# Four of sixteen input loads over fifteen DMA engines, issued from GpSimd, in a store-bound bilinear kernel

## Chip, cores, metric

One core of a Trainium2 chip. The metric is the device time of one execution in microseconds.

## The reference

```python
# r_inputs: (4096, 32, 64) f32,  W: (496, 64, 64) f32
idx_i, idx_j = np.triu_indices(32, k=1)
vi = inputs[:, idx_i, :]
vj = inputs[:, idx_j, :]
vidots = jnp.einsum('bpd,pde->bpe', vi, W)
return vidots * vj                     # (4096, 496, 64) f32
```

The output has 520 MB, the inputs 42 MB.

## The kernel before

A block is 256 batch rows, two on each of 128 partitions; there are sixteen. TensorE multiplies, VectorE (or ACT and GpSimd together) multiplies by the field and fills one of three output buffers `ot`, SP stores it. The next block's input goes into one of two buffers `xs`, issued by ACT for all but the first two blocks:

```python
    xpool = ctx.enter_context(tc.tile_pool(name="xpool", bufs=2))
    opool = ctx.enter_context(tc.tile_pool(name="opool", bufs=3))
    ...
    def load_x(blk, eng, k0=0, k1=NB):
        src = rows_of(x, blk).rearrange("(p k) f d -> p (k f) d", k=NB)
        eng.dma_start(out=xs[blk][:, 1 + k0 * F : 1 + k1 * F, :], in_=src[:, k0 * F : k1 * F, :])
    ...
        if s in loads:
            new_x(loads[s])
            load_x(loads[s], nc.scalar)
    ...
            nc.sync.dma_start(out=...[:, kt, n0 : pa + m, :], in_=ot[:, n0 - base : pa + m - base, :])
```

## Time and profile before

| | before |
|---|---|
| time, median of three runs | 1354.09 us (1353.96 to 1354.46) |
| TensorE, VectorE, GpSimd busy | 87%, 71%, 39% |
| mean DMA rate | 416 GB/s |
| period of a block with an x load, by the last landing record | 82.7 us |
| period of a block without one | 77.9 us |
| sixteenth behind fifteenth landing record, median of the stores issued from 430 to 1250 us | 4.8 us |

The last three rows come from the trace's landing records. Each of the 182 transfers of the kernel before leaves sixteen of them (2912 in all), read here as one for each of the core's sixteen DMA engines, made when that engine's share has landed. They carry no engine number, but their spread tells whether one engine is behind: the sixteenth record's distance from the fifteenth is called the lag below. The profile lines themselves are in the prediction.

### The profile page before, as it was taken

To read this page: it belongs to the slowest core of one execution; us is meant where nothing else is said; L and a number is where in the kernel's file an instruction comes from. 1 tells how busy PE (TensorE), PEld (TensorE's weight loads), DVE (VectorE), ACT (ScalarE), POOL (GpSimd) and SP (SyncE) were. 2 spreads that over 40 slices of the span, in tenths; PEclk is the share of its full clock that TensorE was granted. 3 is DMA by queue.
4 is the path that set the end of the run, shared out by engine and by line. 5 is a ranking of instruction groups with operands and counts; after the bars stand their busy time and mean duration, and the time that the engine had idled before them with its cause. 6 is when DMAs were issued, how large, how long until landed. Compare 5 with 4: busy or idle time off the path is not lost.

```text
span 1353.3 us, 17856 instructions
## 1 busy us (share of the span) xinstructions
PE 1180.3 (87%) x7424; PEld 690.9 (51%) x7424; DVE 956.9 (71%) x1262; ACT 374.1 (28%) x367; POOL 530.2 (39%) x246
## 2 busy tenths in 40 slices
PE   6989889889799897988879989888987989988994
PEld 4556545545455454555445545454554545545552
DVE  5778768767677676776757777676775767767774
ACT  3432222222232232222222222222222222223221
POOL 1813424444243443433444334433434434344431
PEclk9989999989999898999989999899998999989997
DMA  9999999999999999999999999999999999999997
GB/s 386 370 426 408 424 427 431 428 432 431 418 414 419 433 412 418 422 413 426 428 407 422 417 425 410 423 421 407 425 410 426 419 422 427 401 432 428 415 417 319
DMA packets 26273, 562.92 MB, mean 416 GB/s; under 512 B 2912, under 2 KB 2912, under 8 KB 3040
## 3 DMA queue, kind: packets, MB, share of 16 engines
q1 hardware_dynamic: 24048, 530.59, 92.4%
q10 hardware_dynamic: 2144, 31.20, 5.5%
q8 instruction: 58, 0.95, 0.3%
q14 instruction: 23, 0.19, 0.0%
HBM read 41.68 MB, written 520.09 MB: 415 GB/s over the span
## 4 chain that ended last, share of the span: by engine, by line
DMA 50%; PE 25%; DVE 17%; POOL 3%; issue 2%; ACT 0%; DVEq 0%; SPq 0%; POOLq 0%; ACTq 0%
DMA out_dram<-ot 50%; PE ps L211 20%; DVE ot L228 17%; PE ptx L114 4%; POOL ot L226 3%; PE ptw L104 1%; DMA raw<-in_L_rec_W_dram 1%; ACT tmp L225 0%; DVE rp L95 0%; POOL rp L95 0%; DVEq L228 0%; ACT wT L107 0%; SPq L76 0%; POOLq L226 0%; SPq L233 0%
## 5 line engine op out<-in xcount | busy, mean ns | idle before, releaser
L228 DVE TENSOR_TENSOR ot<-ps,xs 128x1024 f32<-128x1024 f32 (+15 forms) x1252 | 945.6, 808 | 364.7 <-DMA out_dram<-ot 185.9
L211 PE MATMUL ps<-wT,xT 64*128 64x512 f32 (+13 forms) x6272 | 1034.9, 473 | 132.8 <-DVE ot L228 121.3
L211 PEld LDWEIGHTS ps<-wT,xT 64*128 64x128 f32 x6272 | 563.7, 197 | 569.9 <-DVE ot L228 306.8
L226 POOL TENSOR_TENSOR ot<-tmp,xs 128x1024 f32<-128x1024 f32 x220 | 519.6, 2362 | 647.4 <-ACT tmp L225 457.1
L225 ACT COPY tmp<-ps 128x1024 f32<-128x1024 f32 x220 | 222.7, 1012 | 500.1 <-PE ps L211 459.6
L118 ACT COPY xT<-ptx 128x1024 f32<-128x1024 f32 x128 | 129.6, 1012 | 428.2 <-PE ptx L114 428.2
L114 PE MATMUL ptx<-ident,xs 128*128 128x128 f32 x1024 | 141.2, 281 | 18.5 <-DVE ot L228 9.9
L114 PEld LDWEIGHTS ptx<-ident,xs 128*128 128x128 f32 x1024 | 111.0, 142 | 64.3 <-issue 44.1
L72 POOL MEMSET xs<- 128x64 f32 x16 | 2.4, 152 | 148.6 <-DVE ot L228 148.6
L104 PE MATMUL ptw<-ident,rp 128*128 128x128 f32 (+1 forms) x128 | 19.2, 305 | 3.9 <-DVE rp L95 3.9
L104 PEld LDWEIGHTS ptw<-ident,rp 128*128 128x128 f32 (+1 forms) x128 | 16.2, 160 | 10.3 <-DVE rp L95 5.0
L107 ACT COPY wT<-ptw 128x1024 f32<-128x1024 f32 (+1 forms) x15 | 14.8, 984 | 21.4 <-PE ptw L104 21.4
L95 DVE COPY rp<-raw 128x1024 f32<-128x1024 f32 (+1 forms) x9 | 10.7, 1219 | 11.1 <-DMA raw<-in_L_rec_W_dram 11.1
L95 POOL COPY rp<-raw 128x1024 f32<-128x1024 f32 x4 | 8.0, 1994 | 0.1
L95 ACT COPY rp<-raw 112x1024 f32<-112x1024 f32 (+1 forms) x3 | 5.9, 1959 | 5.1 <-POOL ot L226 3.3
L107 DVE COPY wT<-ptw 128x1024 f32<-128x1024 f32 x1 | 1.2, 1224 | 3.3 <-PE ptw L104 3.3
L118 ACT ACT_TABLE_LOAD x1 | 1.3, 1283 | 0.7 <-PEq L251 0.7
masks.py:197 POOL MEMSET ident<- 128x128 f32 x1 | 0.2, 206 | 0.3 <-POOLq L251 0.3
masks.py:199 POOL TENSOR_SCALAR_AFFINE_SELECT ident<-ident 128x128 f32<-128x128 f32 x1 | 0.3, 295 | 0.0
L251 POOL MEMSET const-float32-0.0<- 128x1 f32 x1 | 0.1, 99 | 0.2 <-issue 0.2
L251 POOL MEMSET const-bfloat16-1.0<- 128x1 bf16 x1 | 0.1, 102 | 0.0
L251 POOL MEMSET const-uint8-127<- 128x1 uint8 x1 | 0.1, 102 | 0.0
(1 smaller groups left out, 0.1 us busy)
## 6 DMA issues: line engine op xcount, KB each, us to landing
out_dram<-ot SPq DMA_DIRECT2D x64, 3360.0 KB, 16.2
out_dram<-ot SPq DMA_DIRECT2D x32, 3168.0 KB, 15.4
out_dram<-ot SPq DMA_DIRECT2D x32, 3104.0 KB, 17.0
out_dram<-ot SPq DMA_DIRECT2D x31, 2880.0 KB, 16.4
xs<-in_r_inputs_dram ACTq DMA_DIRECT2D x14, 2048.0 KB, 16.6
raw<-in_L_rec_W_dram SPq DMA_DIRECT2D x3, 2048.0 KB, 14.3
xs<-in_r_inputs_dram SPq DMA_DIRECT2D x2, 1024.0 KB, 10.9
xs<-in_r_inputs_dram SPq DMA_DIRECT2D x1, 2048.0 KB, 24.6
```

The source lines that it names most:

```text
L72: nc.gpsimd.memset(xs[blk][:, 0, :], 0.0)
L95: copy(rp[:r], src[:, k * EU : (k + 1) * EU])
L104: nc.tensor.transpose(pt[:, n, :r], rp[:r, n].rearrange("p h d -> p (h d)"), ident[:r, :r])
L107: copy(wT[c][:, :, k * EU : (k + 1) * EU], pt[:, :, :r].rearrange("p e r -> p r e"))
L114: nc.tensor.transpose(pt[:, n, :], xs[blk][:, s : s + 2, :].rearrange("p f d -> p (f d)"), ident)
L118: copy(xT, pt)
L211: nc.tensor.matmul(ps[:, h, lo - pa : hi - pa, :], xT[blk, kt, n // RUN][h * D : (h + 1) * D, n % RUN, :], wT[c][h * D : (h + 1) * D, lo - ...
L225: nc.scalar.copy(tmp, src)
L226: nc.gpsimd.tensor_mul(dst, tmp, xj)
L228: nc.vector.tensor_mul(dst, src, xj)
L251: nc = _bacc.Bacc("TRN2", target_bir_lowering=False, num_devices=1)
```

## The change

The intent is to relieve one of the sixteen DMA engines. 120 of a block's 128 rows go through GpSimd's queue, in two halves by field. The small transfers (`turn_engines`) are there so that the same engine is left out each time. The last eight rows go through ACT's queue, five and three.

No record carries an engine's number, so the numbers in the texts are names. Followed from packet to packet, where the next one starts 3 to 4 ns before the end of the last, the three rows lie in all four loads on three of the engines that carry the five. These three are called 0 to 2, the other two 3 and 4. Number 15 is the name for the engine that 120 rows from ACT's queue are taken to leave out (e4); 5 to 14 are the rest.

```diff
+    SWR = 120
 ...
+    def turn_engines(k: int):
+        n = k if k > 1 else 17
+        c = used[0] % 8
+        used[0] += 1
+        src = x[: NB * n].rearrange("(p k) f d -> p k f d", k=NB)
+        tc.keep_in_program_order(
+            nc.gpsimd.dma_start(out=scratch[:n, :, c : c + 1], in_=src[:, :, 0, 0:1])
+        )
+    def load_fifteen(blk: int):
+        rows = rows_of(x, blk).rearrange("(p k) f d -> p k f d", k=NB)
+        dst = xs[blk][:, 1:, :].rearrange("p (k f) d -> p k f d", k=NB)
+        for a, b in ((SWR, SWR + 5), (SWR + 5, P)):
+            nc.scalar.dma_start(out=xs[blk][a:b, 1:, :], in_=rows[a:b].rearrange("p k f d -> p (k f) d"))
+        for h in range(2):
+            cut = slice(h * F // 2, (h + 1) * F // 2)
+            tc.keep_in_program_order(
+                nc.gpsimd.dma_start(out=dst[:SWR, :, cut, :], in_=rows[:SWR, :, cut, :])
+            )
+            turn_engines(1)
 ...
     load_x(1, nc.sync)
+    turn_engines(5)
 ...
-            load_x(loads[s], nc.scalar)
+            if loads[s] % 3 == 1:
+                load_fifteen(loads[s])
+            else:
+                load_x(loads[s], nc.scalar)
 ... (end of the kernel)
+    turn_engines(11)
```

## The prediction

> **What bounds the kernel now.** I read the page first, then the table by stage, the waits of the store queue, GpSimd's timeline at a block's start, and last the landing records in the trace (each transfer leaves sixteen, one for each DMA engine).

> ```profile
> PE 1180.3 (87%) x7424; PEld 690.9 (51%) x7424; DVE 956.9 (71%) x1262; ACT 374.1 (28%) x367; POOL 530.2 (39%) x246
> ...
> DMA  9999999999999999999999999999999999999997
> ...
> q1 hardware_dynamic: 24048, 530.59, 92.4%
> q10 hardware_dynamic: 2144, 31.20, 5.5%
> ...
> DMA 50%; PE 25%; DVE 17%; POOL 3%; issue 2%; ACT 0%; DVEq 0%; SPq 0%; POOLq 0%; ACTq 0%
> ...
> xs<-in_r_inputs_dram ACTq DMA_DIRECT2D x14, 2048.0 KB, 16.6
> ```

> The DMA engines are busy everywhere, the compute engines are not, and half of the chain that ended last is output transfers. The stores (q1) take 92.4% of the DMA time, the fourteen loads of ACT's queue (q10) 5.5%. So the bytes set the time, and the question is how evenly the sixteen engines carry them.

> ```profile
> 265.00:348.00 83.00, 73.37 (x454) 42.71 (x454) 58.74 (x78) 22.27 (x22) 33.19 (x15) 0.94 1.01 430
> 348.00:431.00 83.00, 72.94 (x462) 43.19 (x464) 58.97 (x80) 22.27 (x22) 33.18 (x15) 0.94 0.99 420
> 431.00:514.00 83.00, 74.14 (x458) 42.86 (x458) 58.99 (x78) 22.27 (x22) 33.18 (x15) 0.94 0.99 418
> ```

> The last two columns are the DMA share and GB/s, one row for each of three blocks of 256 batch rows. In the first the engines never run dry and move 430 GB/s; afterwards they move 418 to 420. The landing records say why. In stores issued between 100 and 200 us the sixteenth record comes a median 0.23 us after the fifteenth; between 200 and 300 us it is 2.3 us, from 430 us on it stays near 4.8 us, while the first fifteen lie within 1.8 us. One engine is slower. Its backlog grows until an output buffer (three) waits for it; then the other fifteen run dry for about 1.1 us in each block (area under the packet records). The slow engine never rests: its landings are evenly spaced by bytes. From its last landings a block with an x load takes 82.7 us (nine of the last ten such blocks within 0.1) and the only later block without one takes 77.9. So **on that engine an x load costs 4.8 us**, its eight rows of 16 KB. A block moves 34.6 MB (32.5 out, 2.1 in); at 430 GB/s the other fifteen would need 80.5 us. They have 2.2 us to spare in each block.

> ```profile
> 348.68 0.15 POOL L72 MEMSET xs<- 128x64 f32 x1 [9.98 <-DVE ot L228]
> 352.08 2.36 POOL L226 TENSOR_TENSOR ot<-tmp,xs 128x1024 f32<-128x1024 f32 x1 [3.25 <-ACT tmp L225]
> 358.62 2.35 POOL L226 TENSOR_TENSOR ot<-tmp,xs 128x1024 f32<-128x1024 f32 x1 [4.17 <-DMA out_dram<-ot]
> ```

> The new GpSimd transfers stand between the first two rows (the instruction order of the changed kernel shows it): there GpSimd waits 3.25 us now, and again 4.17 us before the next product.

> [...] Before, every transfer has 128 or 112 rows and sixteen records[...] This trace has one slow engine with no GpSimd transfer at all, and does not name it.[...]

> **The change, part by part.** Blocks 4, 7, 10 and 13 are loaded in the new way.
> - *Removed:* four loads of 128 rows. The slow engine loses 4 x 4.8 = 19.2 us if it is the one left out.
> - *Added, GpSimd:* twice 120 rows of 4 KB by 2. [...]eight rows on each of fifteen engines, none on the sixteenth. The transfer behind has 17 rows[...]
> - *Cost of the small ones:* 34 elements of 4 bytes on the spared engine. The 4-byte packets in the trace take 9 ns, so 0.3 us of engine time[...]
> - *Added, ACT:* five and three rows, on engines 0 to 4 and 0 to 2. Engines 0 to 2 carry two extra rows, 2 x 0.61 = 1.2 us (x packets take 611 ns): 80.5 + 1.2 = 81.7 us in such a block, still under 82.7. Two issues of 0.35 us instead of one; ACT is 28% busy.
> - *GpSimd's time:* four transfers[...]. 4 to 6 us where it waits 3.25 now: the first product is 1 to 3 us late, four times. The slow engine has some 5 us more queued than the others then, and the next product waits for a buffer anyway: nothing on the path.
> - *The slower landing:* 4 KB packets taking turns with 26.9 KB stores. 32 rounds of 0.15 + 1.0 us are 37 us against 16.6; the next use is some 70 us off. Hidden.

> Sum: 19.2 less 4 to 8, less 1 to 2 for block 4, which is loaded when the backlog is only 2.5 us and cannot give all of 4.8: 9 to 14 us, middle 12.5. 1354.1 - 12.5 = 1341.6, rounded to **1341**. The design closes well: a spared block cuts the backlog by about 4 us, two plain blocks restore 2 x 2.2.

> **The rivals.**
> *The wrong engine is spared.* [...] If the slow engine isn't the spared one, it keeps its eight rows and nothing is won: 1353 to 1357. One in four.
> *The small transfers[...] eat the gain.* If 34 elements cost 2.4 us, two of them take the 4.8 saved: about 1354. The 9 ns speak against it.
> *GpSimd becomes the path.* It is 39% busy, but in-order; if a transfer costs it 3 us or more, its first product is 9 us late in four blocks, more than the backlog: up to 4 x 4 us lost, 1345 to 1360. Its waits of 3.25 and 4.17 us speak against it.
> *More is won.* All bytes at 430 GB/s take 562.9 / 0.430 = 1309 us, plus some 25 us of start: 1334 is the floor with even engines.

> **Range and chances.** If the slow engine is spared (three in four), 1335 to 1348; if not, around 1355. That gives 1333 to 1357. Faster by over 2% means under 1327, below the floor: 0.02. Slower by over 2%, above 1381, takes a stall that none of these sizes gives: 0.03.

> **What would show it.** Right: GpSimd's queue as a third row of the DMA queues with about 7.9 MB; ACT's down by that much; the gap between fifteenth and sixteenth record falls by some 4 us after a spared load and recovers over two blocks; those blocks take 78 to 79 us by last landing, the others 82.7. Wrong: the gap stays near 4.8 us everywhere (another engine is spared), or the spared blocks take 82 us with the gap gone (fifteen engines or GpSimd bound), or GpSimd's first product comes over 5 us late and the store behind it with it.

## The result

The changed kernel takes 1345.61 us (four runs, 1345.58 to 1345.65) against 1354.28 us (four runs). The ratio is 0.9936 (95% interval 0.9919 to 0.9953), 8.7 us less. A ratio here is the mean of one kernel's runs over that of the other's in the same rounds, so not quite the ratio of the medians. By the 2% rule the verdict is "same"; the two sets of times do not overlap.

From the page of the changed kernel, the DMA queues and two groups of GpSimd:

```profile
q1 hardware_dynamic: 24048, 530.59, 93.0%
q10 hardware_dynamic: 1632, 23.33, 4.2%
q0 software_dynamic: 2496, 7.88, 1.5%
...
L92 POOL DMA_DIRECT2D scratch<-in_r_inputs_dram x10 | 9.1, 908 | 0.2 <-issue 0.2
...
L103 POOL DMA_DIRECT2D xs<-in_r_inputs_dram x8 | 6.0, 753 | 1.4 <-issue 1.4
```

GpSimd's queue is the new third row, with the 7.88 MB that ACT's has lost, and issuing the 18 transfers occupies GpSimd for 15.1 us in all. Its timeline at the second of the four loads:

```profile
511.03 0.15 POOL L72 MEMSET xs<- 128x64 f32 x1 [10.04 <-DVE ot L261]
511.54 0.76 POOL L103 DMA_DIRECT2D xs<-in_r_inputs_dram  x1 [0.35 <-issue]
512.30 0.99 POOL L92 DMA_DIRECT2D scratch<-in_r_inputs_dram  x1
513.28 0.74 POOL L103 DMA_DIRECT2D xs<-in_r_inputs_dram  x1
514.02 0.96 POOL L92 DMA_DIRECT2D scratch<-in_r_inputs_dram  x1
515.00 2.37 POOL L259 TENSOR_TENSOR ot<-tmp,xs 128x1024 f32<-128x1024 f32 x1
```

The four issues fit into the wait that stood there before: the first product starts 3.97 us after the memset did, where it was 3.40 us. GpSimd is 0.6 us late, once per load.

The landing records show the aim being met. The two columns are medians of the sixteenth record's lag over the stores issued 50 to 12 us ahead of a load and 25 to 60 us behind it:

| load issued at | lag ahead of it | lag behind it |
|---|---|---|
| 265 us | 1.9 us | 0.8 us |
| 512 us | 4.9 us | 1.3 us |
| 757 us | 4.6 us | 1.4 us |
| 1004 us | 3.8 us | 1.6 us |

By last landing, three consecutive blocks (the spared load and two ACT loads) now take 245.9 to 246.6 us (the shortest: 84.7 + 82.6 + 78.6), where they took 3 x 82.7 = 248.1. A single block's period says little: a GpSimd load lands over some 42 us, all of it behind the boundary at which one period ends, so one block looks short and the next long.

But not everything is gained. In the 46 us behind each load, these are the stages of the changed kernel at three of the four loads; ahead of them one of its ordinary ACT loads (last columns: DMA share, GB/s), and last the kernel before at the same three loads:

```profile
428.00:474.00 46.00, 39.55 (x240) 22.83 (x240) 31.00 (x42) 11.14 (x11) 16.66 (x8) 0.93 1.00 426
510.00:556.00 46.00, 39.61 (x258) 22.63 (x258) 33.55 (x47) 12.47 (x13) 20.74 (x13) 1.00 1.00 412
756.00:802.00 46.00, 39.71 (x256) 22.76 (x258) 33.63 (x47) 12.37 (x13) 20.93 (x13) 1.00 1.00 409
1003.00:1049.00 46.00, 39.68 (x254) 22.42 (x252) 33.53 (x44) 12.15 (x12) 21.41 (x13) 1.00 1.01 413
...
514.00:560.00 46.00, 38.97 (x244) 22.57 (x244) 31.07 (x43) 11.14 (x11) 16.69 (x8) 0.93 0.99 418
762.00:808.00 46.00, 38.84 (x242) 21.82 (x240) 30.87 (x41) 11.14 (x11) 16.68 (x8) 0.96 0.99 421
1010.00:1056.00 46.00, 38.62 (x240) 22.62 (x242) 29.91 (x42) 11.13 (x11) 16.67 (x8) 0.93 0.98 411
```

In the changed kernel the engines never run dry in either kind, but while fifteen of them carry a load they move 409 to 413 GB/s instead of 426 at the three later loads. (At the first, issued at 265 us, where the slow engine has little backlog yet, it is 423.) The kernel before moves 411 to 421 there, with engines that run dry (share 0.98 to 0.99).

Over the whole execution this costs little. The durations of all packet records, added up and divided by sixteen, say how long an engine works on average:

| | span, us | mean busy time of an engine, us | mean idle time, us |
|---|---|---|---|
| before | 1353.3 | 1329.7 | 23.6 |
| the change | 1343.8 | 1330.6 | 13.2 |
| e3 (below) | 1341.9 | 1330.2 | 11.7 |

The work has grown by 1 us at most; the whole gain is idle time that is gone. Successive records of one engine overlap by some 3.5 ns; with that taken off, between 265 and 1250 us an engine is idle for 12.6 us before, 4.3 in the changed kernel and 2.6 in e3. That is the limit which the prediction's sum did not have.

### The profile page after: what moved, and what is told of

Same layout as the page of the kernel before. It is cut to its first block, busy times and chain, and to the rows that moved or that the text cites. A ratio compares the mean times of both kernels' runs of the same rounds, so it can differ in the third digit from the quotient of the medians. Undisturbed runs are those within 1.5% of the kernel's fastest.

```text
span 1343.8 us, 17902 instructions
## 1 busy us (share of the span) xinstructions
PE 1163.9 (87%) x7424; PEld 680.1 (51%) x7424; DVE 956.0 (71%) x1262; ACT 374.1 (28%) x367; POOL 544.7 (41%) x264
## 2 busy tenths in 40 slices
DMA  9999999999999999999999999999999999999997
## 3 DMA queue, kind: packets, MB, share of 16 engines
q1 hardware_dynamic: 24048, 530.59, 93.0%
q0 software_dynamic: 2496, 7.88, 1.5%
## 4 chain that ended last, share of the span: by engine, by line
DMA 50%; PE 23%; DVE 16%; POOL 6%; issue 3%; ACT 1%; DVEq 0%; SPq 0%; POOLq 0%; ACTq 0%
DMA out_dram<-ot 50%; PE ps L244 18%; DVE ot L261 16%; POOL ot L259 5%; PE ptx L143 4%; PE ptw L133 1%; DMA raw<-in_L_rec_W_dram 1%; POOL scratch L92 1%; ACT tmp L258 1%; POOL xs L103 0%; DVE rp L124 0%; POOL rp L124 0%; DVEq L261 0%; ACT wT L136 0%; POOL xs L72 0%
## 5 line engine op out<-in xcount | busy, mean ns | idle before, releaser
L244 PE MATMUL ps<-wT,xT 64*128 64x512 f32 (+13 forms) x6272 | 1017.8, 467 | 122.4 <-DVE ot L261 110.7
L244 PEld LDWEIGHTS ps<-wT,xT 64*128 64x128 f32 x6272 | 552.7, 193 | 553.1 <-DVE ot L261 289.0
L72 POOL MEMSET xs<- 128x64 f32 x16 | 2.4, 151 | 148.5 <-DVE ot L261 148.5
L92 POOL DMA_DIRECT2D scratch<-in_r_inputs_dram x10 | 9.1, 908 | 0.2 <-issue 0.2
L103 POOL DMA_DIRECT2D xs<-in_r_inputs_dram x8 | 6.0, 753 | 1.4 <-issue 1.4
## 6 DMA issues: line engine op xcount, KB each, us to landing
xs<-in_r_inputs_dram ACTq DMA_DIRECT2D x10, 2048.0 KB, 17.3
raw<-in_L_rec_W_dram SPq DMA_DIRECT2D x3, 2048.0 KB, 17.1
```

Source lines behind the costliest of these rows:

```text
L72: nc.gpsimd.memset(xs[blk][:, 0, :], 0.0)
L92: nc.gpsimd.dma_start(out=scratch[:n, :, c : c + 1], in_=src[:, :, 0, 0:1])
L103: nc.gpsimd.dma_start(out=dst[:SWR, :, cut, :], in_=rows[:SWR, :, cut, :])
L244: nc.tensor.matmul(ps[:, h, lo - pa : hi - pa, :], xT[blk, kt, n // RUN][h * D : (h + 1) * D, n % RUN, :], wT[c][h * D : (h + 1) * D, lo - ...
```

## Experiments

Theory A: the gain comes from leaving out the one slow engine. Theory B: it comes from GpSimd's path itself, whose 4 KB packets let stores go first. Each diff is against the changed kernel unless it says otherwise. "Before" was run with every batch (1354.3 to 1355.3 us).

| run | edit | time, us | ratio to before |
|---|---|---|---|
| the change | | 1345.61 | 0.9936 |
| e1 | another engine left out | 1358.51 | 1.0027 |
| e2 | GpSimd, all 128 rows | 1354.87 | 0.9997 |
| e3 | ACT's rows four and four | 1342.98 | 0.9912 |
| e4 | the 120 rows from ACT | 1357.87 | 1.0021 |
| e5, e6 | needless loads | 1409.69, 1410.71 | 1.0405, 1.0412 |
| e7 | e3 with whole rows | 1360.43 | 1.0039 |
| e8 | e3 with seven blocks | 1344.82 | 0.9923 |
| e9 | e3 in four parts | 1343.01 | 0.9915 |
| e10 | e3 cut by batch row | 1357.20 | 1.0019 |
| e11 | e3, last eight rows by GpSimd, whole | 1352.94 | 0.9988 |
| e12 | e11, the eight rows cut by field | 1343.70 | 0.9917 |

**e1: leave out another engine.**

```diff
-    turn_engines(5)
+    turn_engines(6)
-    turn_engines(11)
+    turn_engines(10)
```

> Six rows instead of five in the first small transfer (and ten in the last)[...]. Theory A (the gain comes from leaving out the one slow engine): the gain is lost, 1353 to 1357 us, and the gap between fifteenth and sixteenth landing record stays near 4.8 us. Theory B (the gain comes from GpSimd's path itself, 4 KB packets that let the stores go first): 1345 to 1347 us as now.

Measured 1358.51 us, and the lag stays at a median 4.5 us. One row more in the first small transfer turns a gain of 8.7 us into a loss of 3.6. Most of the loss fits too, by an estimate: if the slow engine is number 4, it now gets eight rows from GpSimd and still one from ACT, nine instead of eight, and 4 x 0.6 = 2.4 us (a 16 KB packet takes 0.61 us). Theory B falls.

**e2: GpSimd without sparing.** `SWR = 128`, no small transfers, no ACT transfer.

> The same four blocks loaded by GpSimd with all 128 rows on sixteen engines, no small transfers, nothing by ACT. Theory A: 1353 to 1357 us, like before or a little slower. Theory B: 1344 to 1347 us.

Measured 1354.87 us, ratio 0.9997, lag 4.9 us. Issuing from GpSimd in 4 KB packets neither costs nor gains anything that shows (95% interval 0.9982 to 1.0012). Its stages at the same three loads:

```profile
514.00:560.00 46.00, 39.53 (x244) 22.45 (x242) 31.89 (x42) 12.02 (x12) 17.98 (x9) 0.96 1.00 419
762.00:808.00 46.00, 39.41 (x244) 22.32 (x242) 31.77 (x42) 11.90 (x12) 17.98 (x9) 0.96 1.00 420
1010.00:1056.00 46.00, 39.23 (x244) 22.11 (x244) 31.31 (x43) 11.14 (x12) 18.14 (x10) 0.96 1.01 424
```

419 to 424 GB/s (426 at the first load), so GpSimd's queue alone explains little of the fall.

**e3: take ACT's row off engine 4.**

```diff
-        for a, b in ((SWR, SWR + 5), (SWR + 5, P)):
+        for a, b in ((SWR, SWR + 4), (SWR + 4, P)):
```

> ACT's eight rows as four and four (engines 0 to 3) instead of five and three (0 to 4 and 0 to 2). If the slow and spared engine is number 4[...], it loses its last row: 4 x 0.6 us, 1343.0 to 1343.6 us. If it is another engine, engine 3 gets one row more and nothing changes: 1345.3 to 1346.0 us.

Measured 1342.98 us, 2.6 us less than the change (3.2 by the ratios, each with its own batch of "before"), as expected if the slow engine is number 4. The edit moves one row from ACT's first transfer to its second. So one 16 KB row on engine 4 costs 0.65 to 0.8 us of the whole time in each load, and the engine that GpSimd leaves out is the slow one. No later version is faster. (e1 to e8 ran on chip 0 by their records, e9 to e11 on chip 3 and e12 on chip 2: the same sparing paid on all three.)

**e4: the 120 rows from ACT's queue**: the same two half transfers issued by `nc.scalar`, no small ones. That they lie on fifteen engines, as GpSimd's do, is taken to be so and not shown.

> The 120 rows issued from ACT's queue[...], no GpSimd transfer. If the slow engine is number 15: 1335 to 1344 us, better than with GpSimd. If not: 1353 to 1357 us, no gain, engines 0 to 2 carry two more rows.

Measured 1357.87 us: nothing is won, so if an engine is left out here, it is not the slow one. Engine 4 would then carry nine rows as in e1 (an estimate: eight of the 120 and one of ACT's five), and they lose 3.0 and 3.6 us. The stages:

```profile
514.00:560.00 46.00, 38.92 (x244) 22.17 (x244) 31.20 (x43) 11.14 (x11) 16.65 (x8) 0.96 0.99 407
762.00:808.00 46.00, 40.87 (x242) 23.18 (x244) 30.92 (x44) 11.35 (x12) 16.66 (x8) 0.89 0.99 400
1012.00:1058.00 46.00, 39.83 (x240) 22.28 (x240) 30.48 (x41) 11.13 (x11) 16.66 (x8) 0.93 0.99 405
```

The same fall of the rate, to 400 to 407 GB/s (422 at the first load), without any GpSimd transfer; a small part of it is engines running dry (share 0.99). It goes with the loads of 120 rows, not with who issues. The nine rows on engine 4 would be a second difference from e2, so this is not shown apart from them.

**e5 and e6: needless loads of four or five rows**, added to the kernel before, to name the slow engine in a second way:

```diff
             load_x(loads[s], nc.scalar)
+            nc.scalar.dma_start(
+                out=raw[3][:4, :],            # e6: [:5, :]
+                in_=rows_of(x, loads[s]).rearrange("(p k) f d -> p (k f d)", k=NB)[:4],
+            )
```

> The kernel before with one needless transfer of four rows of 16 KB behind each of ACT's fourteen x loads[...]. If the slow engine is number 4, these four have 2.2 us to spare in each block and 0.6 us more is hidden: 1354 to 1356.5 us. If the slow engine is one of 0 to 3: about 14 x 0.6 = 8.5 us more, 1362 to 1364 us.

> The same with five rows[...]. If the slow engine is number 4: 14 x 0.6 = 8.5 us more than before, 1361 to 1365 us. If it is any of 5 to 15: as with four rows, within 1 us.

Both failed as experiments: 1409.69 and 1410.71 us. Nothing in the program held the copies in their places, so the scheduler put all fourteen at the front of ACT's queue, where thirteen of them take 55.08 us. From ACT's timeline of e5:

```profile
87.86 55.08 ACTq L189 DMA_DIRECT2D raw<-in_r_inputs_dram  x13
```

ACT stands still for 55 us (56.6 us in e6), as long as the whole difference of 54.8 us. They tell nothing about the engines, and I did not repeat them: e3 had settled the point. The changed kernel's own `keep_in_program_order` is there against just this.

**e7: whole rows**, on top of e3:

```diff
-        for h in range(2):
-            cut = ...
-            ... nc.gpsimd.dma_start(out=dst[:SWR, :, cut, :], in_=rows[:SWR, :, cut, :]) ; turn_engines(1)
+        tc.keep_in_program_order(nc.gpsimd.dma_start(
+            out=xs[blk][:SWR, 1:, :], in_=rows[:SWR].rearrange("p k f d -> p (k f) d")))
+        turn_engines(1)
```

> Four and four rows by ACT as in the third experiment (1343.0 us), and the 120 rows in one GpSimd transfer of whole 16 KB rows with one small transfer behind it. Theory C (the four-byte stand-ins that the spared engine gets in place of each piece stretch its own stores; 32 a load become 8): 1336 to 1340 us. Theory D (a contiguous transfer is split otherwise[...]): 1354 to 1358 us. Theory E (what is lost beside the spared rows does not hang on the number of pieces): 1342 to 1344.5 us.

Measured 1360.43 us. Theories C and E are out for this form. In the packet records the engine left out is recognisable by its four-byte packets, called stand-ins: sixteen in each of the change's eight transfers, as many as each of the fifteen others would have of data (240 / 15). In the changed kernel these stand between stores about 1.03 us apart, 26,880 bytes each: an engine with a backlog, at the slow engine's pace. In e7, from 526.5 us on, they follow each other within some 20 to 40 ns: an engine whose store queue is empty. So a fast engine was left out, as theory D says. The 16 KB packets took 653 ns at the median and 717 on average here, where ACT's take 611 and 644; that may be the 3 us that e7 loses beyond e10, which no run shows.

**e8: seven blocks instead of four**, on top of e3 (`loads[s] % 2 == 1`).

> Four and four rows as in the third experiment, seven of the sixteen blocks instead of four. If the slow engine still sets the pace, each spared load gives the 3.0 us that it gave there: 1333 to 1336 us. If its backlog is used up, so that the other fifteen set the pace in and after a spared load: 1338 to 1342 us.

Measured 1344.82 us (1342.26 to 1346.02), slower than both ranges and not better than four blocks. The lag's median is 1.1 us, and at the loads at 347 and 510 us it is 0.0 to 0.4 us on both sides: the slow engine has no backlog left to give, so the pace is that of all engines. Their mean busy time is 1333.6 us here, 1330.2 in e3. That was the second branch, with its size missed.

**e9: four parts of eight fields**, on top of e3.

> As the third experiment (four and four rows by ACT, 1343.0 us), but the 120 rows in four transfers of eight fields: 2 KB pieces, 64 four-byte stand-ins a load on the spared engine instead of 32, four small transfers instead of two. Theory C (the stand-ins and small transfers stretch the spared engine's stores): some 1 to 2 us more a load, 1347 to 1351 us. Theory F (large pieces make the fifteen engines and the spared one hold each other up, as with whole rows at 1360 us): smaller pieces are no worse, 1340 to 1344 us, unless GpSimd's four more issues of about 0.9 us put its first product late.

Measured 1343.01 us, like e3. The expectation was wrong on what changes: the packets stayed at 4096 bytes (1920 of them, two pieces in each), and so did the number of stand-in packets (now of 8 bytes). What did change is GpSimd's work, eight issues a load instead of four, half of them small transfers; its first product starts 6.4 us after the memset, not 4.0, and the lag's median is 0.5 us, 1.0 in e3. So **neither the small transfers nor GpSimd's issues are on the path**. Theory C in its first form, that stand-ins cost by their number, stays untested.

**e10: cut by batch row**, on top of e3: `out=dst[:SWR, h, :, :], in_=rows[:SWR, h, :, :]`, two transfers with 8 KB contiguous in each row.

> As the third experiment, but cut by batch row instead of by field: two transfers of 120 pieces of 8 KB, 16 stand-ins a load, the same number of small transfers. Theory C: fewer stand-ins, 1339 to 1342 us. Theory F: between the 4 KB pieces (1343.0) and the whole rows (1360), 1346 to 1356 us.

Measured 1357.20 us. The time lies above theory F's range (1346 to 1356) and in the one that e7 gave to D, and the records decide: stand-ins run back to back (eight between 526.55 and 526.62 us), and the median lag behind the three later loads is 3.5 to 4.1 us. Engine 4 was not left out here either.

**e11: the last eight rows by GpSimd**, on top of e3, uncut, with `turn_engines(8)` behind them, nothing by ACT.

> As the third experiment, but the last eight rows by GpSimd[...]; no ACT transfer in these blocks. If engines 0 to 3 with ten rows each set the pace in a spared load: nine rows at most now, 4 x 0.6 us less, 1340 to 1341.5 us. If the pace there is set by something common to all engines: 1342.5 to 1344.5 us; if GpSimd's longer row of issues is on the path: above 1345 us.

Measured 1352.94 us, and the lag explains it: behind the four loads it is 0.5, 4.1, 0.9 and 4.1 us. Only every second load spared the slow engine: with the uncut eight rows and the small transfer behind them, the next load left out another one, and the load after that the slow one again.

**e12: the same with the eight rows cut by field.**

```diff
-        ... nc.gpsimd.dma_start(out=xs[blk][SWR:, 1:, :], in_=rows[SWR:].rearrange("p k f d -> p (k f) d"))
-        turn_engines(8)
+        for h in range(2):
+            cut = slice(h * F // 2, (h + 1) * F // 2)
+            ... nc.gpsimd.dma_start(out=dst[SWR:, :, cut, :], in_=rows[SWR:, :, cut, :])
+            turn_engines(8)
```

> As the run before it with the eight rows by GpSimd, but those too cut by field into two halves, each with a small transfer[...] behind it. Theory D[...]:[...] the slow engine is left out in all four loads, and the gap between fifteenth and sixteenth record falls below 2 us after each, where the run before showed it after the first and third alone. Time: 1340 to 1341.5 us if engines 0 to 3 with ten rows set the pace of a spared load in the third experiment (nine rows at most now); 1342 to 1344.5 us if something common to all engines does. If theory D is wrong[...], nothing changes in the gaps against the run before and the time stays near 1353 us.

Measured 1343.70 us; the lag behind the loads is 0.1, 0.1, 0.5 and 1.1 us. Time and lag are as theory D expected. What the forms tried show (e7, e10 and e11 with one run in each row, the others with two): **120 rows with one run in each did not spare the slow engine (1360.43 and 1357.20 us), cut by field they did (1342.98 us in e3); with the eight rows uncut the slow engine was spared in every second load (lag 0.5, 4.1, 0.9 and 4.1 us), with the eight cut by field in all four (0.1, 0.1, 0.5 and 1.1 us).** Which engine was left out in e7 and e10 is not shown, only that it was not engine 4, nor is what decides it. So the halves by field in the change are not about size: without them the wrong engine is left out. In time e12 equals e3, so the tenth row on engines 0 to 3 (an estimate: eight of the 120 and two of ACT's eight, if its two transfers of four share their engines as the five and three do in the change) did not set e3's pace, unless GpSimd's four more issues took back what it gave; e9, with as many issues, speaks against that.

## Why the prediction was right, and where it was not

The time, 1345.6, lies in the range, the direction and the mechanism hold, and the gain is 70% of the 12.5 us forecast. (The middle of the prediction's own 9 to 14 us is 11.5, and 1341.6 rounds to 1342.) That the number came out is in part luck: a cost that does not exist stood in for a limit that was overlooked.

- *One slow engine sets the pace:* right. e1, e3 and e4 price a row on it at 0.65 to 0.9 us, and the fall and return of the lag are there. **What the others have to spare was mis-sized.** The 2.2 us in each block rest on the 430 GB/s of one stretch; between 265 and 1250 us the engines, while busy, move 424 GB/s, so 34.6 MB need 81.6 us and 1.1 us are to spare. That is what the prediction itself read as their dry time.
- *The spared engine:* I gave three in four that the slow one was meant, an estimate of mine that no trace had shown. The main case was right: it is engine 4, where ACT still puts one of its five rows, and that row was simply a loss. **The term "loses 4 x 4.8 = 19.2 us" was mis-sized** too: seven of eight rows left, and e3 shows 2.6 to 3.2 us still to be had.
- *The small transfers, 4 to 8 us:* **this step failed.** The figure was my estimate and no trace had shown it. Their packets of 136 bytes take a median 46 ns, and e9 doubled their number without cost.
- *What limited the gain instead:* the idle time of the other fifteen. With no row at all on engine 4, e3 saves 11.9 of 19.2 us. Before, the fifteen were idle for 12.6 x 16/15 = 13.4 us between 265 and 1250 us (taking the slow one as never idle), and the rows moved to them cost each 19.2/15 = 1.3 us: an estimate of 12.1 us for the most that sparing can win. e3 has won it; the change keeps a row on engine 4 and falls short of it by about what that row costs. The floor of 1334 us rests on the same 430 GB/s: the bytes kept the engines busy for 1330 us, not 1309.
- *The rate during the loads:* it falls to 409 to 413 GB/s at the three later ones, and I had not expected that. The fall goes with the loads of 120 rows, from either queue (400 to 407 GB/s in e4), and it is not the path through GpSimd (419 to 424 in e2). But the mean busy time grows by only 0.9 us in the change and 1.3 us in e2, so it explains little of what is missing. *Why it falls is open;* no run here separates the causes that it might have.
- *GpSimd:* 0.6 us late instead of 1 to 3, because the four issues take 3.45 us, not 4 to 6, which was my estimate before any run had such an issue. *The landing:* 42 us from first issue to last record, 37 forecast. *The design closes in three blocks:* right, and e8 shows that it does so barely, since sparing more often finds no backlog.

## What to carry to other kernels

Where every DMA engine looks busy, compare the last landing record of a transfer with the one before it: here one engine, 4.8 us behind, set the time of all, and a row moved off it was worth 0.65 to 0.9 us, as long as the others had idle time to give (12.6 us an engine). Before spreading work, find out which engines a transfer really uses; the shape of the access pattern decided that here (1342.98 us in e3, 1357.20 in e10), and a cut that looked like a matter of size was what put the gap in the right place. And price such a step by the idle time of the other engines, not only by the bytes that it takes from the slow one: here 19.2 us were taken away, and about 12 us were all that could be won.
